# The second layer of a loop's first pass cut to one column per block under a condition, and the loop's code laid 12 instructions further on

## The chip, the cores and the metric

The kernel runs on one core of one Trainium2 chip. The metric is the device time of one execution in microseconds. Three runs of the kernel before were taken; their median is 272.04 us.

## What is computed

A layer of a graph network over 12,500 nodes and 412,500 edges (cut to what matters):

```python
h = jnp.maximum(_layernorm(x, axis=-1), 0.0)               # [12500, 128]
agg = jax.ops.segment_sum(edge_attr_48, dst, 12500)        # [12500, 48]
u = graph_globals[zeros]                                   # [12500, 64]
hid = jax.nn.relu(jnp.concatenate([h, agg, u], 1) @ W1 + b1)   # first layer, 256 wide
out = x + (hid @ W2 + b2)                                  # second layer, 128 wide
```

All data are fp32. The edges are sorted by their target node `dst`.

## The kernel before

**Tiling.** Edges come in groups of 4 x 768. A pass of the loop handles 11 groups and 1024 nodes, these as two blocks A and B of 512 nodes (128 partitions by 4 rows). There are 12 passes, a short remainder behind them, and a start ahead of them that turns the targets into offsets. The 11 groups sit in six slots (line 39), most of them with two groups: slots 0 to 2 belong to the first half of a pass, slots 3 to 5 to the second.

**The sum over edges.** For each group VectorE builds one-hot tiles of the targets (`onehots`, L666) and of the groups' places (`places`, L672). TensorE adds up a slot's edges with them (`sums`, L685, in one of two PSUM banks, S0 for even slots and S1 for odd), ScalarE copies the result out (L689), and TensorE places it in the banks of the block (`place`, L707). The bank of slot s is free for slot s + 2 once ScalarE has copied slot s.

**The two layers.** VectorE takes the mean and variance of a block (L714 and on), ScalarE normalizes it (L735), TensorE turns it (L744), ScalarE copies it (L745) and copies the edge sums (`sums_out`, L750). The first layer is `layer_x` (L754) and `layer_e` (L759); ScalarE's `relu` (L764) writes `hid`. The second layer is `second` (L780): for each block 4 rows x 2 halves of `hid`, 8 matmuls, each of them two passes in fp32, so 16 in the profile. VectorE adds the result to `xb` (the block plus b2, made by GpSimd, L739) and keeps it in `hold` (L784).

**The order.** Each operation is listed once by name with what it reads and writes, and the class `Flow` works out the semaphores and writes a loop. Operations are issued on each engine in the order of `body`. The second layer belongs to the blocks of the pass before: it stands behind slots 0 to 2 and their places, ahead of slots 3 to 5. In the first pass there is no block before; `hid` is filled with zeros by ScalarE at the start (`hidz`, `blank`), the full second layer is computed from that, and what VectorE stores of it in `hold` is overwritten later. GpSimd's `add_b` follows VectorE's read of the second layer's result, because it writes `xb` anew; the loads of the next blocks, issued by ScalarE (`load_x`), follow `add_b`; behind these loads, on ScalarE, stand the copies of `sums_out`.

**TensorE's loop.** TensorE has a loop of its own (L243 to L256), cut at `su3`, the sums of slot 3. One turn of it holds, under conditions on its counter j: if j > 0, the second half of the pass before (from slot 3 on); if j < 1, the start; if j < 12, the first half of the next pass (up to the second layer). So the code of the start stands in the middle of the loop's code and is jumped over in the later turns, and the code of the second half is jumped over in the first turn. The other engines share a loop over the 12 passes (L232).

Of the kernel before, what the change touches and what calls it, by code (L numbers as in the profile page):

```python
# [18 lines left out]
P = 128  # L19
# [9 lines left out]
R = 4  # L29
# [25 lines left out]
class Flow:  # L55
# [14 lines left out]
    def op(self, eng, name, reads, writes, emit, dma=False):  # L70
        self.seq.append(dict(eng=eng, name=name, r=tuple(reads), w=tuple(writes), emit=emit, dma=dma, it=self.at))
# [119 lines left out]
    def run(self):  # L191


        lo, hi = self.loop
        nc = self.nc
        start = [o for o in self.seq if o["it"] is None or o["it"] < lo]
        body = [o for o in self.seq if o["it"] == lo]
        end = [o for o in self.seq if o["it"] is not None and o["it"] > hi]
        for e in self.of:
            self.prepare(e)  # L200
        self.straight([o for o in start if o["eng"] != "PE"])
        regs = {}
        for o in body:
            for n, back in self.body.get(o["name"], []):
                u = self.unit(n)
                key = (o["eng"], u, (self.at_lo[n] - lo - back + self.extra[n]) * u)
                if key not in regs:
                    r = self.of[o["eng"]].alloc_register(f"w_{o['eng']}_{len(regs)}")
                    self.of[o["eng"]].reg_mov(r, key[2] + lo * u)
                    regs[key] = r  # L210

        def ahead(e):
            for n, c in sorted(self.ahead[e].items()):
                self.of[e].wait_ge(self.sem[n], (self.rank[n, c] + self.extra[n]) * self.unit(n))

        def repeat(o, i):
            waits = []
            for n, back in self.body.get(o["name"], []):
                u = self.unit(n)
                waits.append((self.sem[n], regs[(o["eng"], u, (self.at_lo[n] - lo - back + self.extra[n]) * u)]))  # L220
            self.emit(o, waits, i)

        def count(e):
            for (f, u, _), r in regs.items():
                if e == f:
                    self.of[e].reg_add(r, r, u)

        others = [e for e in self.of if e != "PE"]
        for e in others:
            ahead(e)  # L230
        every = {o["name"] for o in self.seq if o["it"] == hi}
        with nc.Fori(lo, hi + 1, 1, engines=[self.of[e].engine for e in others]) as i:  # L232
            for e in others:
                mine = [o for o in body if o["eng"] == e]
                for always, some in groupby(mine, lambda o: o["name"] in every):
                    with ExitStack() as last:
                        if not always:
                            last.enter_context(self.of[e].If(i < hi))
                        for o in some:
                            repeat(o, i)  # L240
            for e in others:
                count(e)
        own = [o for o in body if o["eng"] == "PE"]  # L243
        cut = [o["name"] for o in own].index(self.mark)
        with nc.Fori(0, hi - lo + 2, 1, engines=[nc.tensor.engine]) as j:
            with nc.tensor.If(j > 0):
                for o in own[cut:]:
                    repeat(o, None)
                count("PE")
            with nc.tensor.If(j < 1):  # L250
                self.straight([o for o in start if o["eng"] == "PE"])
                ahead("PE")
            with nc.tensor.If(j < hi - lo + 1):
                for o in own[:cut]:
                    repeat(o, None)
        self.straight(end)  # L256


# [149 lines left out]
def kernel(  # L408
# [12 lines left out]
    nc = tc.nc  # L421
# [4 lines left out]
    NH = H // P  # L426
# [19 lines left out]
    def bank(name):  # L446
        return psum.tile([P, BN], F32, name=name)
# [4 lines left out]
    ph = [bank("ph0"), bank("ph1")]  # L452
# [22 lines left out]
    hid = [const.tile([P, NH, r, P], F32, name=f"hid{k}") for k, r in two]  # L475
# [11 lines left out]
    w2 = const.tile([P, NH, D], F32)  # L487
# [25 lines left out]
    f = Flow(nc, tc)  # L513
    op = f.op
    A, B, Z = 0, 1, 2
# [62 lines left out]
    def dst_1(b):  # L578
        rows, n, g0 = dst_shape(b)
        d = di[b]  # L580
        k = f"di{b}"
        src = [k] + ([k + "r", k + "s"] if b == NB - 1 else [])
        op("DVE", f"fc{b}", src, [f"fc{b}"], lambda i: [nc.vector.tensor_copy(fc[b][:rows], d[:rows, 0:1])])
        k = b % DF
        op("DVE", f"df{b}", src + [f"fc{b}"], [f"df{k}"], lambda i: [
            nc.vector.tensor_scalar(df[k][:rows], d[:rows], fc[b][:rows], (V - 1) / 2, OP.subtract, OP.subtract)])
        op("DVE", f"mf{b}", [f"fc{b}", "m4"], [f"mf{b}"], lambda i: [nc.vector.tensor_scalar(mf[b][:rows], m4[:rows], fc[b][:rows], None, OP.mult)])
# [204 lines left out]
    def prologue():  # L792
# [4 lines left out]
        for s in range(NS):  # L797
# [31 lines left out]
        blank = lambda name, key, dst_ap, shape: op("ACT", name, ["zero"], [key], lambda i: [  # L829
            nc.scalar.copy(dst_ap, zero[:shape[0]].to_broadcast(shape) if len(shape) == 2 else zero[:shape[0], :, None].to_broadcast(shape))])  # L830
        op("ACT", "c1", ["eps"], ["sc0"], lambda i: [nc.scalar.activation(sc[0][:, 0:1], eps, AF.Sqrt, bias=eps)])
        for k in (A, B):
            for a in range(NH):
                blank(f"hidz{k}.{a}", f"hid{k}.{a}", hid[k][:, a], [P, R, P])
            blank(f"xbz{k}", f"xb{k}", xb[k], [P, R, D])
        f.chain("DVE", "nm", [], ["nmod_i", "nmod"],
            lambda: nc.vector.tensor_scalar(nmod_i, nmod_i, NV - 1, None, OP.bitwise_and),
# [3 lines left out]
            lambda: nc.vector.tensor_reduce(a4, ident.rearrange("c (g k) -> c k g", k=CG), AX.X, OP.add),  # L841
            lambda: nc.vector.tensor_copy(aq, a4[:, :, None].to_broadcast([P, CG, NV])))
        op("DVE", "c3", ["iota_v"], ["iota_v"], lambda i: [nc.vector.tensor_scalar(iota_v, iota_v, 0.5, None, OP.mult)])
        for b in range(NB):
            dst_1(b)
            dst_2(b)
# [4 lines left out]
                             start=(t == 0), stop=(t == T - 1), skip_group_check=True)  # L851
# [120 lines left out]
    flags = nc.alloc_registers("bad")  # L972
    flag_of = {r.engine: r for r in flags}
    prologue()
    for it in range(NIT):
        body(it)
# [2 lines left out]
    ends = [f"ot{k}" for k in range(3)] + [f"x{k}" for k in (A, B)] + [f"hold{k}.{j}" for k in (A, B) for j in range(NIT - 1)]  # L979
    op("SP", "end", [], ends, lambda i: [nc.sync.nop(nofuse=True)])  # L980
    f.order((0, NIT - 1))
    f.mark = "su3"
    tc.mark_branch_hint_location("skip", engines=[ET.PE, ET.DVE])
    with tc.tile_critical(no_gpsimd_drain=True):
        f.run()
# [33 lines left out]
```

## Time and profile before

| | |
|---|---|
| three runs, us | 272.29, 272.04, 271.69 |
| median, us | 272.04 |
| profiled execution, us | 272.44 |
| its span, us | 270.7 |
| mean granted TensorE clock | 0.976 |
| TensorE matmul busy, share of span | 92% |
| VectorE busy, share of span | 88% |
| ScalarE, GpSimd busy | 47%, 20% |
| bytes moved by DMA | 94.33 MB, 348 GB/s |

Rows of the profile name an engine (PE is TensorE, PEld its weight loads, DVE VectorE, ACT ScalarE, POOL GpSimd, SP SyncE; a q behind it is its DMA issues), a line of the kernel, the operation, what it writes and reads, and how often. In a timeline the first two numbers are the start and the length in us from the span's start; the bracket at the end is the idle time of the engine just before and what ended it. "issue" is idle time that no wait in the profile explains.

### The profile page before, as it was taken

How to read it: one execution, taken by the hardware profiler on the slowest of the kernel's cores; microseconds unless marked ns; L12 is line 12 of the kernel's file. 1: busy time of each engine (PE TensorE's matmuls, PEld its weight loads, DVE VectorE, ACT ScalarE, POOL GpSimd, SP SyncE). 2: the span in 40 equal slices, each digit the busy share in tenths (PEclk: the TensorE clock that was granted, in tenths of full speed). 3: DMA queues.
4: the chain of work that ended last, by engine and by line, in shares of the span. 5: the costliest groups of instructions: out<-in, count | busy, mean ns of one | idle time of the engine just before them, and what ended most of it. 6: DMA issues, size and time to landing. Idle time of an engine off the chain costs nothing.

```text
span 270.7 us, 17205 instructions
## 1 busy us (share of the span) xinstructions
PE 249.3 (92%) x7567; PEld 193.7 (72%) x7568; DVE 239.1 (88%) x591; ACT 127.6 (47%) x316; POOL 54.5 (20%) x47
## 2 busy tenths in 40 slices
PE   0853999999999999999999999999999999999990
PEld 0843894985977958949859769679589498597580
DVE  4699998998998999989989999989999899899511
ACT  6630524644545437337345445364383473454520
POOL 8100050050050230400500501403205005007000
PEclk9996699999999999999999999999999999999997
DMA  6999999999999999999999999999999999979911
GB/s 200 304 390 385 364 387 392 349 390 384 360 392 346 387 393 333 387 393 340 389 393 335 390 351 383 392 339 386 393 330 390 393 336 390 390 246 380 350 41 66
DMA packets 79012, 94.33 MB, mean 348 GB/s; under 512 B 3227, under 2 KB 72189, under 8 KB 78998
## 3 DMA queue, kind: packets, MB, share of 16 engines
q1 hardware_dynamic: 75398, 87.63, 92.4%
q10 hardware_dynamic: 3312, 6.03, 5.8%
q0 software_dynamic: 288, 0.49, 0.7%
q8 instruction: 7, 0.11, 0.2%
q14 instruction: 7, 0.06, 0.1%
HBM read 87.75 MB, written 6.40 MB: 348 GB/s over the span
## 4 chain that ended last, share of the span: by engine, by line
PE 88%; SPq 5%; DMA 3%; issue 1%; DVE 0%
PE s L685 27%; PE ph L780 18%; PE ph L754 8%; PE ax L707 8%; SPq L520 5%; PE ph L759 5%; PE pt L754 4%; PE po L754 4%; PE pt L759 4%; PE ay L707 3%; DMA e<-in_edge_attr_dram 3%; PE pt L744 3%; PE po L744 2%; PE s L942 1%; PE s L754 0%
## 5 line engine op out<-in xcount | busy, mean ns | idle before, releaser
L666 DVE TENSOR_TENSOR oh<-iota_v,rel_i 128x1344 f32<-128x1344 f32 (+1 forms) x78 | 130.5, 1712 | 0.3 <-PE s L685 0.3
L685 PEld LDWEIGHTS s<-e,oh 128*28 128x28 f32 x6336 | 73.2, 108 | 18.5 <-issue 16.4
L685 PE MATMUL s<-e,oh 128*28 128x48 f32 x6336 | 77.7, 208 | 7.5 <-issue 5.8
L739 POOL TENSOR_TENSOR xba<-xa,b_sb 128x512 f32<-128x512 f32 x12 | 15.5, 1290 | 193.6 <-DVE holda L784 193.6
L689 ACT COPY ss<-s 128x96 f32<-128x96 f32 (+1 forms) x72 | 17.0, 236 | 65.8 <-PE s L685 65.8
L672 DVE TENSOR_SCALAR pl<-iota_w,off_i 128x186 f32<-128x186 f32 x141 | 35.0, 308 | 0.5
L739 POOL TENSOR_TENSOR xbb<-xb,b_sb 128x512 f32<-128x512 f32 x12 | 31.1, 2594 | 0.0
L764 ACT ACTIVATE hida<-ph,bias 128x512 f32<-128x512 f32 x12 | 8.2, 687 | 41.4 <-PE ph L759 41.4
L780 PEld LDWEIGHTS ph<-w,hida 128*128 128x128 f32 x208 | 24.8, 195 | 3.9 <-issue 3.9
L707 PE MATMUL ax<-pl,ss 128*48 128x186 f32 (+3 forms) x172 | 27.3, 300 | 0.0
L780 PE MATMUL ph<-w,hida 128*128 128x128 f32 x208 | 27.3, 285 | 0.0
L707 PE MATMUL ay<-pl,ss 128*48 128x186 f32 (+3 forms) x168 | 26.4, 298 | 0.0
L780 PE MATMUL ph<-w,hidb 128*128 128x128 f32 x208 | 25.4, 275 | 0.0
L780 PEld LDWEIGHTS ph<-w,hidb 128*128 128x128 f32 x208 | 24.3, 192 | 0.0
L707 PEld LDWEIGHTS ax<-pl,ss 128*48 128x48 f32 x172 | 17.6, 126 | 4.3 <-issue 2.0
L735 ACT ACTIVATE xna<-xa,sha,sca 128x128 f32<-128x128 f32 x48 | 19.8, 484 | 1.0 <-DVE sha L731 1.0
L735 ACT ACTIVATE xnb<-xb,shb,scb 128x128 f32<-128x128 f32 x48 | 19.6, 481 | 0.0
L707 PEld LDWEIGHTS ay<-pl,ss 128*48 128x48 f32 x168 | 17.8, 124 | 0.0
L714 DVE BATCH_NORM_STATS2 sta<-xa 128x6 f32<-128x128 f32 x48 | 10.5, 280 | 6.1 <-DMA xa<-in_x_dram 6.1
L759 PE MATMUL ph<-ags,w1a 48*128 48x512 f32 x48 | 13.5, 641 | 0.0
L754 PE MATMUL ph<-hta,w1h 128*128 128x512 f32 x24 | 13.5, 645 | 0.0
L754 PE MATMUL po<-htb,w1h 128*128 128x512 f32 x24 | 12.3, 592 | 0.0
(150 smaller groups left out, 300.2 us busy)
## 6 DMA issues: line engine op xcount, KB each, us to landing
e<-in_edge_attr_dram SPq DMA_DIRECT2D x133, 576.0 KB, 7.7
xa<-in_x_dram ACTq DMA_DIRECT2D x11, 256.0 KB, 5.3
xb<-in_x_dram ACTq DMA_DIRECT2D x11, 256.0 KB, 5.8
out_dram<-holda SPq DMA_DIRECT2D x11, 256.0 KB, 3.5
out_dram<-holdb SPq DMA_DIRECT2D x11, 256.0 KB, 3.5
holda<-in_dst_dram SPq DMA_DIRECT2D x4, 384.0 KB, 5.0
e<-in_edge_attr_dram SPq DMA_DIRECT2D x1, 720.0 KB, 4.3
xa<-in_x_dram SPq DMA_DIRECT2D x1, 256.0 KB, 9.5
```

The lines of the kernel that those rows point to most:

```text
L520: return [f.of[eng].dma_start(dst_ap(i) if callable(dst_ap) else dst_ap, src_ap(i) if callable(src_ap) else src_ap)]
L666: op("DVE", f"oh{name}", reads + ["iota_v"], [f"oh{name}"], lambda i: [nc.vector.tensor_tensor(ov, iota_v[:, None, None, :].to_broadcast([ ...
L672: nc.vector.tensor_scalar(out[:, j], iota_w, o[j], None, OP.is_equal) for j in range(len(o))])
L685: nc.tensor.matmul(S[k][NV * c:NV * c + V, j * DE:(j + 1) * DE], o[:, (j * CG + c) * T + t], ev[:, j * CG + c, t * DE:(t + 1) * DE], start ...
L689: op("ACT", f"ss{name}", [f"S{k}"], [f"ss{name}"], lambda i: [nc.scalar.copy(sv.rearrange("p j d -> p (j d)"), S[k][:, :m * DE])])
L707: out.append(nc.tensor.matmul(agg[bk][h:h + DE, at:at + w], sv[:, j], pv[:, j, frm:frm + w], start=bk in fresh and bk not in seen, stop=Tr ...
L735: nc.scalar.activation(xn[k][:m, r], xt[k][:m, r], AF.Relu, bias=sh[k][:m, r:r + 1], scale=sc[k][:m, r:r + 1]) for r in range(RR[k])])
L739: nc.gpsimd.tensor_tensor(xb[k][:m], xt[k][:m], b2_sb[:m, None, :].to_broadcast([m, RR[k], D]), OP.add)])
L744: op("PE", f"tu{k}", [f"xn{k}", "ident"], [key], lambda i: [nc.tensor.transpose(pv[:, r, :m], xn[k][:m, r], ident[:m, :m]) for r in range( ...
L754: nc.tensor.matmul(o, w1h[:, a * P:(a + 1) * P], hT[k][:, :, :m], start=first, stop=False, skip_group_check=True)])
L759: nc.tensor.matmul(o, w1a[h:h + DE, a * P:(a + 1) * P], ag[k // 2][h:h + DE, :, :m], start=False, stop=True, skip_group_check=True)])
L780: nc.tensor.matmul(ov[:m, r], hid[k][:, a, r, :m], w2[:, a], start=(a == 0), stop=(a == NH - 1)) for r in range(RR[k]) for a in range(NH)])
```

## The change

Four edits.

1. TensorE's loop gets `head_slot`: instructions are fetched in pages of 256, and the loop's first instruction is laid at place 86 of its page. That is 12 further than before; the space is padding that is jumped over.
2. In the first half, operations that have a brief form are put under two conditions: at j < 1 the brief form is issued, at j > 0 the full one. The two second layers (A and B) stand next to each other and share the two conditions.
3. The brief form of a second layer is one matmul: the first 128 x 128 tile of `hid` as weights and a single column of W2, written to the first column of the block's PSUM bank.
4. At the start ScalarE fills only that tile of `hid` with zeros for each block, not all 8 tiles. VectorE fills the two banks `ph` with zeros (`phz`), since the brief form leaves most of them unwritten.

```diff
-        with nc.Fori(0, hi - lo + 2, 1, engines=[nc.tensor.engine]) as j:
+        with nc.Fori(0, hi - lo + 2, 1, engines=[nc.tensor.engine], head_slot={nc.tensor.engine: self.slot}) as j:
             with nc.tensor.If(j > 0):
                 for o in own[cut:]:
                     repeat(o, None)
...
             with nc.tensor.If(j < hi - lo + 1):
-                for o in own[:cut]:
-                    repeat(o, None)
+                for brief, some in groupby(own[:cut], lambda o: o["name"] in self.brief):
+                    some = list(some)
+                    if not brief:
+                        for o in some:
+                            repeat(o, None)
+                        continue
+                    with nc.tensor.If(j < 1):
+                        for o in some:
+                            repeat(dict(o, emit=self.brief[o["name"]]), None)
+                    with nc.tensor.If(j > 0):
+                        for o in some:
+                            repeat(o, None)
...
-            for a in range(NH):
-                blank(f"hidz{k}.{a}", f"hid{k}.{a}", hid[k][:, a], [P, R, P])
+            blank(f"hidz{k}", f"hid{k}.0", hid[k][:, 0, 0], [P, P])
...
+        op("DVE", "phz", [], ["PH0", "PH1"], lambda i: [nc.vector.memset(ph[k], 0.0) for k in (A, B)])
...
-    f.mark = "su3"
+    f.mark, f.slot = "su3", 86
+    f.brief = {f"w2{k}": lambda i, k=k: [nc.tensor.matmul(ph[k][:, 0:1], hid[k][:, 0, 0], w2[:, 0, 0:1], start=True, stop=True)] for k in (A, B)}
```

## Prediction

> **What bounds the kernel now.** I read the page first, then the chain of waits, then the table by stretches, then the first pass in the timeline.
>
> ```profile
> PE 249.3 (92%) x7567; PEld 193.7 (72%) x7568; DVE 239.1 (88%) x591; ACT 127.6 (47%) x316; POOL 54.5 (20%) x47
> q8 instruction: 7, 0.11, 0.2%
> L685 PE MATMUL s<-e,oh 128*28 128x48 f32 x6336 | 77.7, 208 | 7.5 <-issue 5.8
> xb<-in_x_dram ACTq DMA_DIRECT2D x11, 256.0 KB, 5.8
> ```
>
> TensorE is the busiest engine and VectorE is close behind. Queue q8 carried 7 packets of instructions, 0.11 MB, so 16 KB each, in the whole run: TensorE's program is fetched once, page by page, and the passes of the loop refetch nothing.
>
> ```profile
> 31.21 4.35 PE ph L780 x32
> 35.56 2.74 PE s L685 x240
> 50.62 3.77 PE ph L780 x32
> 54.39 2.74 PE s L685 x240
> 73.23 2.74 PE s L685 x240
> ```
>
> The chain (start, length, work) runs through TensorE alone. The same work comes back every 73.23 - 54.39 = 18.84 us. L780 is the second layer; in the first pass it multiplies the blank tiles and takes 4.35 us. Its end (54.39) is the start of the next sums: the loop's back edge, with its counter, branches and waits, costs TensorE nothing there.
>
> ```profile
> 22.14:32.38 10.24, 6.47 (x159) 5.38 (x146) 9.91 (x34) 3.00 (x9) 0.00 (x0) 0.50 1.09 371
> 32.38:42.62 10.24, 10.24 (x297) 8.65 (x297) 9.91 (x16) 4.17 (x11) 3.83 (x2) 1.00 1.08 387
> 28.97:32.38 3.41, 3.41 (x25) 2.68 (x20) 3.34 (x7) 2.19 (x7) 0.00 (x0) 0.50 1.09 357
> 50.62:69.46 18.84, 18.84 (x614) 14.51 (x613) 17.97 (x44) 9.51 (x26) 3.84 (x2) 1.00 1.07 375
> ```
>
> By stretches (length, then busy time of PE, PEld, DVE, ACT, POOL, granted clock, DMA share, GB/s): a later pass is 18.84 us of TensorE in 18.84, VectorE 17.97. So time taken out of TensorE in the first pass stays out to the end, unless something in the first two passes is then late. From 22.14 to 32.38 TensorE had half its clock.
>
> ```profile
> 4.17 0.15 DVE L583 CAST fc<-holda 128x1 f32<-128x1 int32 x1 [1.23 <-DMA holda<-in_dst_dram]
> 7.57 0.50 PEld L593 LDWEIGHTS s<-mf,aq 128*128 128x128 f32 x2 [7.25 <-issue]
> 11.25 0.61 DVE L586 TENSOR_SCALAR holda<-holda,fc 26x768 f32<-26x768 int32 x1 [0.78 <-PE pt L600]
> 15.59 0.60 PE L860 MATMUL ph<-u,w1u 64*128 64x1 f32 x4
> 16.60 1.22 PE L685 MATMUL s<-e,oh 128*28 128x48 f32 x95 [0.41 <-DMA e<-in_edge_attr_dram]
> 21.15 1.76 PE L685 MATMUL s<-e,oh 128*28 128x48 f32 x97 [3.33 <-issue]
> 24.19 0.85 PE L685 MATMUL s<-e,oh 128*28 128x48 f32 x29 [1.27 <-DMA e<-in_edge_attr_dram]
> 24.75 7.71 SPq L520 DMA_DIRECT2D e<-in_edge_attr_dram  x6
> 27.53 1.64 PE L685 MATMUL s<-e,oh 128*28 128x48 f32 x67 [2.50 <-issue]
> ```
>
> Up to here the first pass waits for data and, at 21.15 and 27.53, for a page of instructions ("issue"): between the two stops lie 97 + 29 = 126 matmuls, each with its weight load, and 4 waits, 256 instructions of 64 bytes, one packet of 16 KB. The pages are waited for only in this pass.
>
> ```profile
> 31.14 2.63 PE L780 MATMUL ph<-w,hida 128*128 128x128 f32 x16
> 32.01 1.63 ACT L735 ACTIVATE xnb<-xb,shb,scb 128x128 f32<-128x128 f32 x4
> 35.84 0.68 DVE L784 TENSOR_TENSOR holdb<-ph,xbb 128x512 f32 x1
> 36.01 1.28 POOL L739 TENSOR_TENSOR xba<-xa,b_sb 128x512 f32<-128x512 f32 x1 [28.04 <-DVE holda L784]
> 36.78 0.24 ACT L689 COPY ss<-s 128x96 f32<-128x96 f32 x1 [3.14 <-PE s L685]
> 37.26 2.58 POOL L739 TENSOR_TENSOR xbb<-xb,b_sb 128x512 f32<-128x512 f32 x1
> 39.64 0.40 ACTq L520 DMA_DIRECT2D xa<-in_x_dram  x1
> 40.23 0.40 ACTq L520 DMA_DIRECT2D xb<-in_x_dram  x1
> 40.68 0.58 ACT L750 COPY ags<-ax 48x512 f32<-48x512 f32 x1 [0.69 <-PE ay L707]
> 41.28 0.58 ACT L750 COPY ags<-ay 48x512 f32<-48x512 f32 x1
> 44.13 1.13 PE L759 MATMUL ph<-ags,w1a 48*128 48x512 f32 x4
> 45.03 0.87 DVE L714 BATCH_NORM_STATS2 sta<-xa 128x6 f32<-128x128 f32 x4 [1.03 <-DMA xa<-in_x_dram]
> 46.49 0.87 DVE L714 BATCH_NORM_STATS2 stb<-xb 128x6 f32<-128x128 f32 x4
> ```
>
> These rows hold the answer: what ScalarE, GpSimd and VectorE do while TensorE multiplies zeros.
>
> **The change part by part.** *Removed and added on TensorE.* 32 matmuls, 4.35 us of the chain, become 4 (two products of fp32, two passes each, as L860's two make four). L860's four, one column each, took 0.60 us at full clock; at half clock at most twice that. I take 0.65, near the row, since a column is short either way. The sums of slot 3 then start at 31.14 + 0.65 = 31.8, not 35.56. Until 32.38 they run at half clock (67 in 1.64: 24 ns each, so 24 of their 96), the rest at 240 in 2.74 (11.4 ns): issued by 33.2, and with the 208 ns of one matmul to the last result, 33.4. So far 3.5 us are gained.
>
> *What is late next: ScalarE.* Its copy of slot 3's sums (36.78) must follow the norm of B, which ends at 32.01 + 1.63 = 33.64 whatever TensorE does. The copy ends at 33.88, and slot 5, in the same bank, starts behind it; before, behind 36.78 + 0.24 = 37.02. The gain falls to 3.1 us.
>
> *Then GpSimd.* The first layer's second half (L759) reads two copies that ScalarE makes behind the load of xb, and that load waits for GpSimd's xbb, which ends at 37.26 + 2.58 = 39.84. That does not move: it follows VectorE's holdb (35.84), and VectorE reaches that by its own work (9.91 us busy in the stretch of 10.24). So: load issued 39.85 to 40.25, copies to 40.88 and 41.49, TensorE's B half at 41.55. Moved by 3.1 us, L759 would stand at 41.0; it is held to 41.55. Gain: 44.13 - 41.55 = 2.6 us.
>
> *The second pass*:
>
> ```profile
> 49.47 0.48 PE L707 MATMUL ax<-pl,ss 128*48 128x140 f32 x3
> 50.55 2.05 PE L780 MATMUL ph<-w,hida 128*128 128x128 f32 x16
> 60.23 0.58 ACT L750 COPY ags<-ay 48x512 f32<-48x512 f32 x1
> 62.96 0.30 PEld L759 LDWEIGHTS ph<-ags,w1a 48*128 48x128 f32 x4 [0.76 <-issue]
> DMA to landing us min/median/max: 6.2/8.8/10.0
> ```
>
> There L759 comes at 62.96 - 2.6 = 60.4, and its copy must be ready: now it ends at 60.81. It comes 0.6 earlier: xa's load goes out at 37.3 behind xba (36.01 + 1.28), not at 39.64, so VectorE's wait of 1.03 goes; next late is xb, issued 0.37 earlier, with 5.8 to 6.0 us to landing at 45.9, where VectorE waited until 46.49. Copy at 60.2, 0.2 us to spare. If xb lands no earlier, TensorE loses up to 0.4 there. Of the edge loads, the one that slot 5 of the first pass reads went out first in the row at 24.75 and lands, by 6.2 to 10.0 us, from 31.0 to 34.8; as the first of six I take it for there by 33.9, and if it comes last, 0.9 us are waited, of which 0.55 is slack ahead of L759. Those of the second pass, issued by 40.3 and landed within 10.0 us (50.3), are read from 51.7 on, the last of them at 53.3. Later passes loosen, VectorE and DMA needing less than 18.84 us.
>
> *The two branches in every pass* stand between 12 matmuls of L707 and L780. The 12 fill 49.47 to 50.55; their 24 instructions, at the rate of the sums (480 in 2.74 us) are handed out in 0.14 us, so 0.9 us of queued work covers the branches, as at the back edge. I take 0. The upper bound is the only stretch where TensorE stood among branches with nothing queued: from 16.19 (L860's end) to 16.60, 0.41 us, which holds a wait for data too; 12 times that is 4.9 us. [...]
>
> *Twelve instructions further on.* Both stops come 6 matmuls earlier in the code, leaving 6 more behind them (0.07 and 0.15 us); the page ahead of them is entered earlier too, which may give up to 0.3 back. Both are hidden while slot 3 ends by 33.6 (33.4 above). The jump over the padding comes ahead of TensorE's first instruction (7.57), on which VectorE waits at 11.25, so all that follows may be late by it: 0 to 0.2, I take 0.1. The loop's last instruction stood at 225 of its page (134 + 1 + 24 + 64 + 2 after the stop at 27.53); with 12 and the 10 new ones it stands at 247 of 256.
>
> *At nothing:* VectorE's two fills of ph lie in its idle 1.23 us ahead of 4.17, at most 2 x 0.68 by the row of holdb; TensorE takes that result only at 7.57. ScalarE's shorter blanks end in idle time.
>
> **Sum.** -2.6 + 0.1 = -2.5 us. The profiled execution took 272.44 us (span 270.7), giving 269.9; from the median of 272.04 it gives 269.5.
>
> **The rivals.** *Branches bare, slower:* if TensorE's queue is empty when it meets the two branches, each of 12 passes pays. From 2.6 / 12 = 0.22 us a pass the gain is gone; at 0.3 it is 272.0 - 2.5 + 3.6 = 273.1. Against it speaks the back edge at 54.39. *Join on the next page:* nine slots are left by my count; if the loader puts the place where the branch over the second layer lands on the next page, the first pass waits for that page. Pages came 6.4 us apart (21.15, 27.53), so at about 34, and the back edge behind it makes 34.6: gain 0.9, 271.1. *Clock stays low:* if the short matmuls leave the clock at 0.50 past 32.38, half of TensorE's work in that time is lost, on which 3.5 - 2.6 = 0.9 is slack: for 3.4 us more, the length of the last stretch before it rose, 1.7 - 0.9 = 0.8, so 270.3; for as long again as the row says (10.24), 5.1 - 0.9 = 4.2, so 273.7. Against it: the full rate followed on a stretch (28.97 to 32.38) in which TensorE was busy throughout, and it still will be. [...] *Nothing else late:* without the waits on ScalarE and GpSimd, 3.6 us: 268.4.
>
> **How the numbers follow.** Forecast 0.66; branches bare 0.05; join on the next page 0.11 (the change would then do only a third of what it says); clock low 0.08 for the short time and 0.02 for the long one; nothing late 0.08. The likeliest gives 269.5, by its bounds 269.1 to 270.2. The range is 268.6 to 271.3, which takes in the clock and the join. A measurement here tells apart some 0.2%, 0.54 us: faster means below 271.5. Faster 0.89: forecast, nothing late, the short low clock and most of the join; same 0.05: the rest of the join and some of the branches; slower 0.06.
>
> **What would show it.** L780 in the first pass 4 long; the sums of slot 3 at about 31.8; the copy of slot 3 at 33.6 right behind xnb; xbb ending at 39.8 as now; the copies of ay at 40.9; L759 about 41.5; the passes 18.84 apart. Wrong if the passes grow longer, if a stop by "issue" over 1 us follows 31.8, or if L759 waits in the second pass for more than 0.5 us.

## The result and the profile after

The changed kernel takes 283.14 us (median of 4, 280.75 to 284.55) beside 272.17 us of the kernel before (median of 4, 271.69 to 273.11): a ratio of 1.039 with a 95% interval of 1.0307 to 1.0472. It is slower by 11 us, where 2.5 us less were forecast. The profiled execution took 284.55 us (span 282.8, mean granted clock 0.939), that of before 272.44 (270.7, 0.976); the difference of the spans, 12.1 us, is what has to be explained. Lines of the changed kernel stand ten further down: the sums are L695, the second layer L790, the four short matmuls L993.

The page of the changed kernel:

```profile
PE 252.5 (89%) x7539; PEld 195.9 (69%) x7540; DVE 239.9 (85%) x593; ACT 126.3 (45%) x314; POOL 53.6 (19%) x47
...
PEclk9965756999999999999999999999999999999797
...
q8 instruction: 14, 0.23, 0.3%
...
PE 85%; SPq 5%; issue 4%; DMA 3%; DVE 0%
...
L695 PE MATMUL s<-e,oh 128*28 128x48 f32 x6336 | 81.1, 212 | 14.6 <-issue 12.2
```

Queue q8 now carries 14 packets of instructions instead of 7, 4% of the chain is "issue", and the matmuls of the sums had 12.2 us of waiting for "issue" ahead of them instead of 5.8. When the packets came is seen from the table of DMA queues, cut to the stretch from 28 to 64 us; first the changed kernel, then the kernel before:

```profile
q8 instruction: 7, 0.11, 1.3%
```

```profile
q8 instruction: 1, 0.02, 0.2%
```

In the first 28 us there are 4 packets in both, and from 64 to 240 us none. So six pages come again, in the second turn of TensorE's loop, and in no later one. The chain of the changed kernel (start, length, work) shows what they cost:

```profile
25.00 1.55 issue
26.55 1.76 PE s L695 x74
...
30.14 0.54 PE ph L993 x4
30.67 1.05 PE s L695 x83
31.72 3.56 issue
35.28 2.78 PE s L695 x127
38.06 3.46 issue
41.53 0.86 PE s L695 x30
...
52.31 2.65 PE s L695 x210
54.96 1.73 issue
56.69 1.01 PE s L695 x72
...
58.79 3.77 PE ph L790 x32
62.56 2.74 PE s L695 x240
...
81.40 2.74 PE s L695 x240
...
269.34 1.98 PE ph L790 x16
...
274.12 0.42 DVE otr L792
```

Up to 30.67 the change does what it says: the second layer of the first pass is 0.54 us, and the sums of slot 3 start 4.9 us earlier than before (35.56). Of these, 3.8 us are the shorter layer (4.35 - 0.54); the rest is that TensorE reaches it at 30.14 instead of 31.21. Then TensorE stands three times, 3.56 + 3.46 + 1.73 = 8.75 us. The first stop comes 83 matmuls behind the loop's head: 86 slots, 83 times a matmul and its weight load, and 4 instructions of the head make 256, the end of the head's page. The second comes 127 such pairs and 2 waits later, 256 again. These are the ends of the loop's pages, met in order. From 62.56 on the passes are 81.40 - 62.56 = 18.84 us apart, as before: later turns fetch nothing. By stretches (length, busy time of PE, PEld, DVE, ACT, POOL, granted clock, DMA share, GB/s):

```profile
29.87:33.21 3.34, 1.85 (x91) 1.51 (x88) 3.31 (x6) 3.19 (x8) 0.00 (x0) 1.00 1.09 362
33.21:46.86 13.65, 8.11 (x182) 6.91 (x182) 9.61 (x18) 2.62 (x7) 3.82 (x2) 0.50 1.07 382
46.86:62.56 15.70, 13.97 (x353) 9.90 (x356) 10.85 (x34) 6.88 (x18) 0.89 (x1) 1.00 0.67 224
258.60:265.30 6.70, 6.70 (x91) 3.68 (x90) 3.61 (x21) 3.71 (x9) 0.00 (x0) 1.00 0.94 348
265.30:268.70 3.40, 3.40 (x10) 2.19 (x9) 0.00 (x0) 0.57 (x2) 0.00 (x0) 0.50 0.03 10
```

From 33.21 on, within the first stop, TensorE has half its clock (0.50) for 13.65 us. The last two rows lie in the epilogue, where 3.4 us at half clock fall on the last first layer. The end of the chain before, for comparison:

```profile
259.73 1.98 PE ph L780 x16
...
264.51 0.43 DVE otr L782
```

The 12.1 us are three terms. Up to the third turn of TensorE's loop, which begins with the sums of slot 3 of the second pass: 62.56 - 54.39 = 8.17 us. From there to the epilogue's second layer: 269.34 - 259.73 = 9.61, so 1.44 more, the half clock of the epilogue (the kernel before has 1.00 from 258 to 268). From the last result to the end of the span: 282.8 - 274.12 = 8.68 against 270.7 - 264.51 = 6.19, 2.49 more. In that last stretch the changed kernel fetches two pages where the kernel before fetches one, and the program's last jump, over the fallback code `general`, takes 3.71 us instead of 0.35.

### The profile page after: what moved, and what is told of

It is laid out like the page before. It is cut to its first block, busy times and chain, and to the rows that moved or that the text cites. A ratio compares the mean times of both kernels' runs of the same rounds, so it can differ in the third digit from the quotient of the medians.

```text
span 282.8 us, 17174 instructions
## 1 busy us (share of the span) xinstructions
PE 252.5 (89%) x7539; PEld 195.9 (69%) x7540; DVE 239.9 (85%) x593; ACT 126.3 (45%) x314; POOL 53.6 (19%) x47
## 4 chain that ended last, share of the span: by engine, by line
PE 85%; SPq 5%; issue 4%; DMA 3%; DVE 0%
PE s L695 27%; PE ph L790 16%; PE ph L764 8%; PE ax L717 7%; SPq L530 5%; PE ph L769 4%; PE po L764 4%; PE pt L764 4%; PE pt L769 4%; PE ay L717 3%; DMA e<-in_edge_attr_dram 3%; PE pt L754 3%; PE po L754 2%; PE s L952 1%; PE s L764 1%
## 5 line engine op out<-in xcount | busy, mean ns | idle before, releaser
L695 PE MATMUL s<-e,oh 128*28 128x48 f32 x6336 | 81.1, 212 | 14.6 <-issue 12.2
L695 PEld LDWEIGHTS s<-e,oh 128*28 128x28 f32 x6336 | 76.3, 110 | 25.7 <-issue 24.0
L749 POOL TENSOR_TENSOR xbb<-xb,b_sb 128x512 f32<-128x512 f32 x12 | 29.8, 2482 | 0.4 <-DVE holdb L794 0.4
L717 PE MATMUL ay<-pl,ss 128*48 128x186 f32 (+3 forms) x168 | 27.4, 306 | 0.0
L790 PEld LDWEIGHTS ph<-w,hida 128*128 128x128 f32 x192 | 22.3, 191 | 3.4 <-issue 3.4
L790 PE MATMUL ph<-w,hida 128*128 128x128 f32 x192 | 24.6, 281 | 0.0
L790 PE MATMUL ph<-w,hidb 128*128 128x128 f32 x192 | 23.4, 275 | 0.0
L790 PEld LDWEIGHTS ph<-w,hidb 128*128 128x128 f32 x192 | 22.4, 192 | 0.0
L717 PEld LDWEIGHTS ay<-pl,ss 128*48 128x48 f32 x168 | 18.5, 128 | 0.1
L769 PE MATMUL ph<-ags,w1a 48*128 48x512 f32 x48 | 13.5, 641 | 0.0
L764 PE MATMUL ph<-htb,w1h 128*128 128x512 f32 x24 | 12.3, 592 | 0.0
```

Of the source, the lines that this page charges most:

```text
L695: nc.tensor.matmul(S[k][NV * c:NV * c + V, j * DE:(j + 1) * DE], o[:, (j * CG + c) * T + t], ev[:, j * CG + c, t * DE:(t + 1) * DE], start ...
L717: out.append(nc.tensor.matmul(agg[bk][h:h + DE, at:at + w], sv[:, j], pv[:, j, frm:frm + w], start=bk in fresh and bk not in seen, stop=Tr ...
L749: nc.gpsimd.tensor_tensor(xb[k][:m], xt[k][:m], b2_sb[:m, None, :].to_broadcast([m, RR[k], D]), OP.add)])
L764: nc.tensor.matmul(o, w1h[:, a * P:(a + 1) * P], hT[k][:, :, :m], start=first, stop=False, skip_group_check=True)])
L769: nc.tensor.matmul(o, w1a[h:h + DE, a * P:(a + 1) * P], ag[k // 2][h:h + DE, :, :m], start=False, stop=True, skip_group_check=True)])
L790: nc.tensor.matmul(ov[:m, r], hid[k][:, a, r, :m], w2[:, a], start=(a == 0), stop=(a == NH - 1)) for r in range(RR[k]) for a in range(NH)])
```

## The experiments

Two things can be read for each run without any theory: how many packets of instructions came between 28 and 64 us (1 in the kernel before, 7 in the changed one), and where the sums of slot 3 start in the third turn of TensorE's loop (54.39 and 62.56; the recorded expectations call this the third half). Both are read from the one profiled execution of each run. Line numbers differ from run to run; the work is named in the rows. All times are us; the ratio is to the kernel before, run beside it.

| run | what it is | packets, 28 to 64 | third turn | median | ratio, 95% interval |
|---|---|---|---|---|---|
| brief_only | brief layer, no head_slot | 1 | 51.54 | 269.93 | 0.9929 [0.9896, 0.9962] |
| slot_only | head_slot 86 alone | 7 | 63.95 | 282.53 | 1.0382 [1.0319, 1.0445] |
| wait_end | changed kernel, late back edge | 7 | 62.95 | 284.58 | 1.0466 [1.0406, 1.0526] |
| ifs_alone | conditions, whole layer | 1 | 54.16 | 280.90 | 1.0335 [1.0270, 1.0401] |
| moves12 | came out as brief_only | 1 | 51.73 | 269.83 | 0.9924 [0.9899, 0.9948] |
| slot77 | brief, head_slot 77 | 7 | 62.82 | 281.69 | 1.0337 [1.0281, 1.0394] |
| jump_no_align | brief, short jump ahead of the loop | 7 | 59.94 | 279.76 | 1.0284 [1.0225, 1.0343] |
| late_jump | changed kernel, jump 3.5 us later | 8 | 64.92 | 285.02 | 1.0478 [1.0437, 1.0520] |
| incs12 | brief, slot 86 without a jump | 1 | 55.47 | 275.97 | 1.0121 [1.0071, 1.0171] |
| jump_in_loop | brief, short jump as the loop's first act | 7 | 62.82 | 282.74 | 1.0360 [1.0290, 1.0431] |
| swap | brief, start laid ahead of the second half | 2 | 55.36 | 274.00 | 1.0048 [0.9999, 1.0097] |
| swap_jump | swap, short jump ahead of the loop | 2 | 55.00 | 275.46 | 1.0085 [1.0023, 1.0147] |
| jump_gap | jump_no_align, 12 increments behind the jump | 1 | 55.44 | 275.50 | 1.0101 [0.9990, 1.0212] |
| swap_jump_at_leap | swap, short jump at the leap | 2 | 54.34 | 273.65 | 1.0055 [1.0004, 1.0106] |

**First four: which part of the change, and is it the early back edge?** The theory after reading the trace (A) was this. With the brief layer the back edge of the first turn comes at 28.7 us, before the page behind the loop's last has landed (its packet runs from 30.6 to 31.7); before, it came at 33.5, behind that packet; so a back edge taken while a page is on its way loses the pages held. The rivals: the move to slot 86 (B), the two conditions (C).

brief_only, slot_only and wait_end, in this order:

```diff
-        with nc.Fori(0, hi - lo + 2, 1, engines=[nc.tensor.engine], head_slot={nc.tensor.engine: self.slot}) as j:
+        with nc.Fori(0, hi - lo + 2, 1, engines=[nc.tensor.engine]) as j:
```

> The change without the move: the loop's head stays where it was in its page, the second layer of the first pass is brief. Theory A (the back edge of the first turn comes while the next page of TensorE's program is still on its way, and the pages held are lost with it): the second turn still stands by 'issue' three times or so, 7 to 9 us in all, 12 to 14 instruction packets instead of 7, third half's sums of slot 3 near 62.5, time 280 to 284. Rival B (the move to slot 86 is what no longer fits): no such stops, 7 packets, 269 to 272. Rival C (the two conditions cost the pages, in whatever turn): as A, 280 to 284. About the end: if only the length of the program sets where its last label lies, ten instructions fewer than in the changed kernel; the jump at the end takes 3.7 us where that still crosses a page, 0.4 us where it doesn't.

```diff
 (the kernel before)
-        with nc.Fori(0, hi - lo + 2, 1, engines=[nc.tensor.engine]) as j:
+        with nc.Fori(0, hi - lo + 2, 1, engines=[nc.tensor.engine], head_slot={nc.tensor.engine: 86}) as j:
```

> The kernel before with the loop's head moved 12 instructions on and nothing else: the whole second layer in every pass, no condition. Theory A: the back edge comes at 33.5 as before, behind the page that was on its way (31 to 33 us), so 7 packets, no stop by 'issue' over 1 us in the second turn, and 271.5 to 272.5; up to 274.7 if the twelve instructions alone bring the label at the end into another page. Rival B: the stops of the changed kernel, 12 to 14 packets, 279 to 284. Rival C: as A.

```diff
 (the changed kernel; the end of TensorE's first half of a pass)
                     with nc.tensor.If(j > 0):
                         for o in some:
                             repeat(o, None)
+                nc.tensor.wait_ge(self.gate, 1)   # gate: raised by the norm of block B
```

> The changed kernel, with one wait more at the end of TensorE's first half of a pass: for the normalisation of block B on ScalarE in the first pass, which ends at 33.6 (true at once in every later pass). Both conditions, the brief layer and slot 86 stay; only the back edge of the first turn comes later, at 33.6 to 33.9. Theory A: the page on its way is in by then, so 7 or 8 packets, no stop by 'issue' over 1 us in the second turn, sums of slot 3 from about 34.2 (before: 35.5), third half's near 53.2 (before: 54.4), and 270.5 without and 273 with the 2.5 us at the end that the longer program costs. Rivals B and C: the stops stay or grow, 283 to 288.

In ifs_alone every pass does the four short matmuls once and then all of the second layer, so it multiplies a little more than the reference needs:

```diff
 (the kernel before; its loop over the first half grouped as in the change, and the fill `phz` added)
+                    if brief:
+                        for when in (j < 1, j > 0):
+                            with nc.tensor.If(when):
+                                for o in some:
+                                    self.brief[o["name"]](None)
                     for o in some:
                         repeat(o, None)
```

> The kernel before with the two conditions put in ahead of the whole second layer, each around the four short matmuls alone, so that every pass does the short ones and then all of the second layer; head where it was. Theory A: the back edge of the first turn comes at 33.5 to 34.5, behind the page on its way; 7 packets, no stop by 'issue' over 1 us in the second turn; each pass about 0.6 us longer for the short matmuls, 13 times at most 8 us, so 272 to 280, but with the third half's sums of slot 3 only 1.2 us later than before (near 55.6). Rival C: the pages are fetched again, 12 to 14 packets, third half's sums past 62. Rival B: as A.

Theory A falls on all sides. In brief_only the back edge comes at 28.67, in the middle of the packet (28.54 to 29.73), and nothing is fetched again. In slot_only and wait_end it comes at 33.4, when the packet has landed (by 32.25 and 31.20), and six pages are fetched again. What goes with the loss is head_slot, with or without the brief layer. The chain of slot_only:

```profile
35.43 1.05 PE s L685 x83
36.48 3.28 issue
39.76 2.78 PE s L685 x127
42.53 1.27 issue
```

The stops are at the same ends of pages, behind 83 and 127 matmuls, with the whole second layer in place. Rival C falls with brief_only, which has both conditions in every turn. The profiled execution of ifs_alone (276.73) says the same, with 1 packet and the third turn at 54.16; each later pass is 0.45 us longer. Its other executions took 279.75 to 282.68 and have no profile, so its ratio is not read as the price of the conditions.

**Second four: the slot, or the jump that leads to it?** head_slot does two things: it moves the loop's head, and it has TensorE jump over the padding in front of it. Theory D: the jump loses the pages. Rival B: the place does.

```diff
 (the changed kernel without head_slot)
+        still = nc.tensor.alloc_register("still")
+        for _ in range(12):
+            nc.tensor.reg_mov(still, 0)
         with nc.Fori(0, hi - lo + 2, 1, engines=[nc.tensor.engine]) as j:
```

> The changed kernel without head_slot: instead, twelve register moves are put ahead of the loop, so its head lies at the same slot 86 but is reached without the jump over a padding (0.18 us at 1.75 us in the changed kernel). Theory D (the jump taken just ahead of the loop loses the page that follows it, page 1; the second turn then finds it missing and takes it and all behind it one at a time): no stop by 'issue' over 1 us in the second turn, 5 packets up to 40 us, and about 269 to 270.5 for the loop, plus 1 us for the moves (12 at 0.09) and 2.5 us at the end if the label there crosses a page: 269 to 273. Rival B (the slot itself: what counts is how the loop lies in its pages): the stops of the changed kernel, 11 packets up to 62 us, 281 to 285.

This one misses its point: the trace shows none of the twelve moves. Nobody reads the register, which is probably why they fell out of the program. It is brief_only a second time, and agrees with it (269.83, 1 packet).

```diff
-    f.mark, f.slot = "su3", 86
+    f.mark, f.slot = "su3", 77
```

> The changed kernel with head_slot 77 instead of 86: the loop lies within three instructions of where it lies without a head_slot (74), but is reached through a jump over a padding. Theory D: pages 1 to 6 are fetched again in the second turn, 11 packets up to 62 us, 280 to 284. Rival B: as with the head left in place, 5 packets up to 40 us, 269.5 to 271.

```diff
 (the changed kernel without head_slot)
+        still = nc.alloc_registers("still", engines=[nc.tensor.engine])
+        nc.regs_mov(still, 0)
+        with nc.tensor.If(nc.snap(still, min_val=0, max_val=1) > 0):
+            nc.tensor.reg_mov(nc.tensor.alloc_register("never"), 0)
         with nc.Fori(0, hi - lo + 2, 1, engines=[nc.tensor.engine]) as j:
```

> The brief layer with the head left in place and no padding, but a condition that is never met around one register move just ahead of the loop: a taken jump over one instruction. Theory D in its plain form (any jump taken there): pages 1 to 6 are fetched again, 280 to 284. If it takes the padding itself, or rival B: 5 packets up to 40 us and 269.5 to 271.

```diff
 (the changed kernel)
+        first = [o for o in start if o["eng"] == "PE"][0]
+        for d in first["waits"]:
+            nc.tensor.wait_ge(self.sem[d["name"]], self.value(d))
         with nc.Fori(0, hi - lo + 2, 1, engines=[nc.tensor.engine], head_slot={nc.tensor.engine: self.slot}) as j:
```

> The changed kernel with a wait ahead of the jump over the padding: for what TensorE's first transposes wait for anyway (about 7.4 us), so that the jump comes 5.5 us later, and the loop's first page is asked for that much later too. Theory D, if the loss comes of page 1 being still on its way when the jump is taken (a page takes 4 to 6 us here): 5 packets up to 45 us, no stop by 'issue' over 1 us in the second turn, 272 to 278 (the start 3 to 5.5 us later, what of it the other engines hide not known). Theory D without that condition, or rival B: the stops stay and the start is later, 285 to 289.

The jump is needed for it. With the head three instructions from where it lies without head_slot, the loss is there (slot77); with no padding at all and a jump over one instruction, it is there (jump_no_align). The chain of jump_no_align:

```profile
32.66 1.91 PE s L699 x88
34.56 1.91 issue
36.48 2.77 PE s L699 x127
39.25 2.38 issue
...
52.72 1.41 issue
54.13 0.96 PE s L699 x69
...
59.94 2.74 PE s L699 x240
```

late_jump takes the jump at 5.26 us instead of 1.75 and loses the pages just the same (8 packets: one of the first turn's has moved behind 28 us). Call the page with the loop's head page 0; in the first turn a long jump, the leap, goes from it over page 1 to the start's code on page 2. In no run is there a packet between the start of the program and the leap (the leap begins at 2.07 us in the changed kernel and the first packet at 4.42; before, 1.84 and 5.01), and swap_jump below runs page 1 without a packet for it. I infer that page 1 was held from before the program's start; no row shows the pages held as such. A request for it in the jump's way is unlikely, then.

**Third four: what the jump must stand before.** In the first turn the loop's head is followed by a long jump: the second half of a pass is skipped, and page 1 with it. D1: a short jump ahead of that leap loses the pages. D2: it matters that the head is entered by a jump. The first run of the four gives slot 86 without a jump.

```diff
 (the changed kernel without head_slot)
+        spare = self.tc.alloc_semaphore("spare")
+        for _ in range(12):
+            nc.tensor.sem_inc(spare, 1)
         with nc.Fori(0, hi - lo + 2, 1, engines=[nc.tensor.engine]) as j:
```

> The changed kernel without head_slot; twelve increments of a semaphore that nobody reads stand ahead of the loop, so that its head lies at slot 86 and is reached without a jump. Theory D (a jump taken on the head's page ahead of the loop loses the pages): 5 packets of TensorE's program up to 40 us, no stop by 'issue' over 1 us in the second turn, sums of slot 3 a little later than with the head left in place (the increments take some 0.09 us each, 1.1 us in all, ahead of the first page's request), 270 to 271.5; at the end the program is as long as the changed one, so the last jump takes 3.4 to 3.7 us instead of 0.4 and the time is 273 to 274 if length alone moves the last label onto another page. Rival B (the slot): 11 packets up to 62 us, 281 to 285.

```diff
 (the same, without the increments; never is a register that holds 0)
         with nc.Fori(0, hi - lo + 2, 1, engines=[nc.tensor.engine]) as j:
+            with nc.tensor.If(never > 0):
+                nc.tensor.sem_inc(spare, 1)
             with nc.tensor.If(j > 0):
```

> The brief layer, head left in place, and a condition that is never met around one increment as the loop's own first instructions: the jump is taken in every turn, behind the head, on the head's page, and in the first turn ahead of the long jump to the start's page. Theory D1 (what does it is any short jump on that page ahead of the long jump, which leaps over page 1): pages 1 to 6 fetched again in the second turn, 11 packets up to 62 us, 279 to 285. Theory D2 (what does it is that the loop's head is entered by a jump): 5 packets up to 40 us, the jump itself 0.23 us by 13 turns, in part hidden, 270 to 273.

```diff
 (the changed kernel without head_slot)
+            with nc.tensor.If(j < 1):
+                self.straight([o for o in start if o["eng"] == "PE"])
+                ahead("PE")
             with nc.tensor.If(j > 0):
                 for o in own[cut:]:
                     repeat(o, None)
                 count("PE")
-            with nc.tensor.If(j < 1):
-                self.straight([o for o in start if o["eng"] == "PE"])
-                ahead("PE")
```

> The brief layer, no head_slot, and in the loop the start (first turn only) laid ahead of the second half of the pass before, so that the first turn runs on from the head into page 1 and leaps from there, over pages 1 and 2. No jump ahead of the head. Theories D1 and D2: no page is fetched twice; 5 to 6 packets in the first turn and none in the second but for pages never run yet (1 or 2, page 2 above all); the first transposes may begin at 5.2 to 6 instead of 7.2 since their page is there, and a stop of 4 to 6 us comes behind the start instead, at the leap: 266 to 274.

```diff
 (swap)
+        with nc.tensor.If(never > 0):
+            nc.tensor.sem_inc(spare, 1)
         with nc.Fori(0, hi - lo + 2, 1, engines=[nc.tensor.engine]) as j:
```

> As e11_swap, with the jump of e7_jump_no_align ahead of the loop. D1 in the form 'page 1 is lost and the long jump leaps over it': page 1 is now run, and so fetched, in the first turn, one packet and a stop more there; the second turn then goes as without the jump, 267 to 276, within 0.7 to 5 us of e11_swap. D2, or any loss that the jump ahead of the loop brings to the back edge whatever the order inside: in the second turn the pages are fetched one after the other again, 5 packets more than e11_swap has and 7 to 12 us longer.

incs12 ends rival B: slot 86 reached without a jump loses nothing. Its 276 us are two other things. The increments take 0.15 us each, not the 0.09 expected, so that the first page is asked for 1.8 us later (3.65 instead of 1.85 in brief_only); its packet then begins 4.9 us behind the leap instead of 3.0. TensorE's first matmuls come 3.9 us later than in brief_only, and the third turn is at 55.47, as much behind. And the end is long. The last rows of its chain and the packets behind 240 us:

```profile
265.58 0.42 DVE otr L795
```

```profile
q8 instruction: 3, 0.05, 0.3%
```

Its span is 274.2, so 8.6 us follow the last result, as in the changed kernel; brief_only has 267.8 - 261.56 = 6.2 and 2 packets there. The third packet, and the 2.5 us, occur in just the five longest programs (the changed kernel, wait_end, late_jump, incs12, jump_gap: 22 instructions or more ahead of the end beyond those of before) and in none of those with some 10 to 15 more. So that term goes with the program's length: incs12 has it without the jump, brief_only has the brief layer without it.

jump_in_loop has the short jump behind the head and in every turn; it loses the pages in the second turn like the changed kernel, and in no later one. That fits D1 and not D2. swap and swap_jump have the same 2 packets between 28 and 64 us, first fetches of the pages behind the leap, which comes later there (at 15.48 and 16.07); the short jump shows no cost. So a short jump on the head's page doesn't itself lose page 1: in swap_jump TensorE runs on from it into page 1 and finds it there, with no packet for it (the first one starts at 19.3 us, behind the leap; five packets in 40 us are pages 2 to 6). The leap right behind it is needed too.

**Last two: what in the pair.** In every losing run the leap starts less than 0.5 us behind the short jump (0.33 in the changed kernel, slot_only, wait_end, slot77 and late_jump, 0.29 in jump_in_loop, 0.47 in jump_no_align). The two branches of the changed kernel, on TensorE's queue (shortest, median and longest time in ns, then the first and last start):

```profile
L245 PEldq COMPARE_BRANCH  x1: 176/176/176, 1.7 to 1.7; - x1
L246 PEldq COMPARE_BRANCH  x1: 4708/4708/4708, 2.1 to 2.1; - x1
```

The first is the short jump; the second is the leap, 4.71 us long, in which the first packet of q8 comes (4.42 to 5.36). The last two runs ask whether the distance counts, and whether the page does.

```diff
 (jump_no_align, with an increment as the instruction that is jumped over)
         with nc.tensor.If(never > 0):
             nc.tensor.sem_inc(spare, 1)
+        for _ in range(12):
+            nc.tensor.sem_inc(spare, 1)
         with nc.Fori(0, hi - lo + 2, 1, engines=[nc.tensor.engine]) as j:
```

> As e7_jump_no_align (head left in place, brief layer, a short jump ahead of the loop), with the twelve increments of e9_incs12 between the short jump and the loop: the short jump is taken at 1.85 us and the long one, over page 1, some 1.9 us later instead of 0.47. If what loses the pages is two jumps close together (in every losing run so far the second came within 0.5 us of the first): one packet from 28 to 64 us, as in e9_incs12, and 275 to 277 with its late start and long last jump. If the short jump on the head's page ahead of the leap is enough, whatever lies between: seven packets from 28 to 64 us, and 285 to 290.

```diff
 (swap)
             with nc.tensor.If(j < 1):
                 self.straight([o for o in start if o["eng"] == "PE"])
                 ahead("PE")
+                with nc.tensor.If(never > 0):
+                    nc.tensor.sem_inc(spare, 1)
```

> As e11_swap, with the short jump as the last thing of the start, so that it comes right ahead of the leap, on page 1, which the first turn has entered; the leap goes over page 2, which has been asked for but not run. If two jumps close together, the second over a page not yet run, lose it and what follows: page 2 and those behind it are fetched again in the second turn, six packets or more from 28 to 64 us instead of two, and 280 to 286. If the loss hangs on page 1 (held since before the program's start, and leapt over): two packets, 273 to 275.

With 2.3 us between the short jump (1.84) and the leap (4.17), nothing is lost. The two branches of jump_gap, its packets between 28 and 64 us, then its chain:

```profile
L249 PEldq COMPARE_BRANCH  x1: 227/227/227, 1.8 to 1.8; - x1
L254 PEldq COMPARE_BRANCH  x1: 5596/5596/5596, 4.2 to 4.2; - x1
```

```profile
q8 instruction: 1, 0.02, 0.2%
```

```profile
34.69 4.65 PE s L703 x240
...
55.44 2.74 PE s L703 x240
```

The 240 matmuls of the sums that follow the back edge run without a stop (4.65 us, at a granted clock of 0.55), where jump_no_align stood twice. Twelve increments lie in the gap as well as 2.3 us; which of the two counts these runs do not tell, nor what happens between 0.47 and 2.3 us. And closeness isn't all: in swap_jump_at_leap the pair is 0.42 us apart, on page 1, with page 2 leapt over, and nothing is fetched twice. (swap itself has a branch of 0.32 us at 15.10, 0.38 us ahead of its leap, longer than the branches that fall through, 0.07 to 0.09; it loses nothing either.) swap_jump_at_leap changes the page and its state together: page 2 had not been held since the start. Shown is this much: in the seven runs that have, on the loop's head page, a short jump 0.29 to 0.47 us ahead of the leap over the next page, six pages are fetched again in the second turn (7 packets between 28 and 64 us instead of 1; 8 in late_jump, one of them from the first turn). What TensorE's sequencer does with the pages in that moment, whether page 1 must be one not yet entered or not fetched by a packet, and why pages 2 to 6, which it had fetched itself, go too, stays open.

## Why the prediction was wrong

**Right, as brief_only shows.** The forecast's main sum stood on the brief layer; without the jump it comes out at 269.93 us, beside 269.5 forecast; the kernel before took 272.31 in the same batch, and the ratio is 0.9929. Rows of its first pass in the timeline (start, length, engine, work; the idle time ahead in brackets):

```profile
29.87 0.38 PE L993 MATMUL ph<-w,hida 128*128 128x1 f32 x2
...
30.41 1.74 PE L695 MATMUL s<-e,oh 128*28 128x48 f32 x144
...
31.81 1.64 ACT L745 ACTIVATE xnb<-xb,shb,scb 128x128 f32<-128x128 f32 x4
...
33.35 0.31 ACT L699 COPY ss<-s 128x96 f32<-128x96 f32 x2
...
34.10 1.22 PE L695 MATMUL s<-e,oh 128*28 128x48 f32 x96 [1.95 <-DMA e<-in_edge_attr_dram]
...
35.64 0.68 DVE L794 TENSOR_TENSOR holdb<-ph,xbb 128x512 f32 x1
...
37.06 2.58 POOL L749 TENSOR_TENSOR xbb<-xb,b_sb 128x512 f32<-128x512 f32 x1
...
40.65 0.58 ACT L760 COPY ags<-ay 48x512 f32<-48x512 f32 x1
...
41.16 1.25 PE L769 MATMUL ph<-ags,w1a 48*128 48x512 f32 x4
```

Short matmuls: 30.41 - 29.87 = 0.54 us (forecast 0.65). Copy of slot 3 at the end of the norm of B: 33.35 (33.6). The load that slot 5 reads lands last, at 34.0 (named as "if it comes last"), so it is this load that holds slot 5, and ScalarE's copy was done 0.35 us before it (33.66). xbb ends at 39.64 (39.84), the last copy at 41.23 (41.49), L769 at 41.16 (41.55): the gain there is 44.13 - 41.16 = 3.0 us. The third turn starts 54.39 - 51.54 = 2.85 us earlier, and the span is 270.7 - 267.8 = 2.9 us shorter, where 2.6 were forecast for the loop. GpSimd was late next, as the prediction had it, and the branches cost nothing: the passes stay 18.84 us apart (51.54 to 70.38). That the clock would return is right too: the 144 matmuls of the sums from 30.41 on take 1.74 us, 12.1 ns each, near the 11.4 ns of 240 in 2.74 at full clock; in the changed kernel the clock is at 1.00 from 29.87 to 33.21.

Part of this agreement is luck. The sums of slot 3 start at 30.41, not at 31.8: TensorE reaches the second layer 1.27 us earlier than before, and the last page ahead of it had come earlier too (from 24.14 instead of 25.15). The forecast doesn't have that; the waits behind it hide it. And xbb comes 0.2 us earlier than before because VectorE's holdb does (35.64 instead of 35.84), where the prediction said that this "does not move"; without these 0.2 us the gain is near 2.65, the 2.6 forecast.

**Wrong: the step "Twelve instructions further on".** It put the jump over the padding at 0 to 0.2 us, taken as 0.1, for its length and its place ahead of the first transposes. The jump itself takes 0.18 us and delays nothing that follows: TensorE starts at 6.97 in the changed kernel, 0.6 us earlier than before. What it does is to the pages, a turn later. Under that step lay the sentence "the passes of the loop refetch nothing" and "The pages are waited for only in this pass": read from 7 packets in a trace that had one jump fewer, and carried over as if it belonged to the loop. It hung on the jumps that TensorE takes in the first turn. Price: from the start of slot 3's sums in the second turn to that in the third it is 31.89 us instead of 18.83, so 13.06 more; 8.75 of these are stops, and the other 4.3, in which the half clock lies, were not split. Less the 4.9 us gained ahead of them, that leaves the 8.17 us at the third turn. slot_only, with nothing of the brief layer, gives 1.0382, as much as the whole change.

The 1.44 us of half clock in the epilogue are not part of that price. From the third turn to the epilogue's second layer the kernel before takes 205.3 us; slot_only, wait_end, jump_no_align and late_jump, which lose the pages too, take 205.2 to 205.3, and only slot77 and jump_in_loop show a longer time, 207.1 to 207.2, beside the changed kernel's 206.8. What brings it stays open.

The long jump back brings no fetch by itself. The 7 pages from the head to the one behind the loop are 112 KB by their packets of 16 KB, and the back edge goes back over five of them in every turn; yet between 64 and 240 us there is no packet of q8 in either kernel, in brief_only or in swap_jump, and their passes are 18.84 us apart, to within 0.1. Measured, only the second turn pays, and only behind the pair of jumps.

**Wrong by omission: the end.** The step counted slots up to the loop's end (247 of 256) and looked there for a place on the next page; the same count wasn't made for the code behind the loop. The twelve and the ten instructions make its last jump wait for a page: 2.5 us, which incs12 has without the short jump.

**Wrong: the rivals.** None moved a cost to the second turn. "Branches bare" had the right sign and the wrong mechanism. "A stop by issue over 1 us follows 31.8" was named as what would prove the forecast wrong; it did, with 3.46 and 1.73 us, behind the one of 3.56 that begins at 31.72.

## What to carry to other kernels

Count the packets of instructions by stretches of the loop, not only in all, and ask of each change to the code ahead of a loop what it does to the pages held, above all when it adds a jump close to another one that leaps over a page (0.29 to 0.47 us ahead of it here). When a change has two parts, each has to be costed as if it came alone: here one gains 2.9 us and the other loses 10. When instructions are added, find the next page boundary behind every one of them, down to the last jump of the program.

## What the runs showed of the hardware that was not expected

- With a short taken jump 0.29 to 0.47 us ahead of the leap over the next page, TensorE fetched six pages again, one turn of the loop later (7 packets between 28 and 64 us instead of 1); with 2.3 us and 12 increments between the two (1 packet), or with such a pair 0.42 us apart on the next page (2, both first fetches), it did not.
- Such a loss cost stops of up to 3.6 us at three or four page ends of one turn (3.56, 3.46 and 1.73 in the changed kernel). There the clock was at 0.50 for 13.65 us, from 33.21, within the first of them, to 46.86.
- One increment of a semaphore on TensorE took 0.15 us from start to start ahead of the loop (incs12), a register move 0.09 (1.24, 1.33 and 1.42 us in the changed kernel).
- With the start's code laid right behind the head (swap), the first transposes begin at 5.17 us instead of 7.57; the stop moves to the leap behind them, 6.6 us, and the time is about that of the kernel before.
